# A four-layer network on one core: split subtractions on GpSimd, later transfers, and stages joined by halves

## The chip, the core and the metric

The kernel runs on one core of one Trainium2 chip. The metric is the device time of one execution in microseconds; lower is better. The engines are named as in the profile: PE (matrix products), PEld (its weight loads), DVE (VectorE), ACT (ScalarE), POOL (GpSimd) and SP, whose queue issues most transfers. All matrix products are float32 unless said otherwise.

## What is computed

The input x is 8 images of 256 channels of 32 x 32 pixels. Four layers follow, cut here to what matters:

```python
# layer 0: batch norm, attention over 1024 pixels (16 heads, key size 16, value size 64), MLP
q, k, v = wq @ bn(x) + bq, wk @ bn(x) + bk, wv @ bn(x) + bv
x = x + wp @ (softmax(q.T @ k * 4) @ v) + bp
x = x + w2 @ relu6(w1 @ bn(x) + bb1) + bb2
# layer 1: 1x1 convolution to 64 channels, deformable 3x3 convolution, 1x1 back
h = relu(bn(w1 @ x)); off, mask = split(conv3x3(h, woff) + boff)
h = bilinear(h, places + off) * sigmoid(mask)      # 9 taps of 4 corners
x = relu(bn(w3 @ relu(bn(w2 @ h))) + x)
# layer 2: sign(x) convolved 3x3 with sign(weights), batch norm over all images, added to x
x = x + bn(scaling * conv3x3(sign(x), sign(weights)))
# layer 3: conv3x3 to 128 channels, silu, depthwise 3x3, layer norm, gelu, offsets and masks,
#          deformable sampling of a 5x5 window, output product, silu, added to x
```

Batch norms of layers 0 and 2 need statistics over all images, so the stages are: attention, a middle stage (the MLP, layer 1 and layer 2's convolution), and layer 3.

## The kernel before, in words

x stays in SBUF as two tiles of 128 channels for 8 images of 1024 pixels; a half is 512 pixels.

**Attention.** Work goes by groups of four heads of an image (32 groups), each in two blocks of 512 queries, each block in NT = 8 steps of 128 keys. The order is written by hand: `plan(step, place, f, ...)` puts a piece of work into a step, and `step(t)` issues the scores and exponentials of the next keys (`exps`), the value products and sums of exponentials (`attend`; the additions of esum run on POOL), four score maxima of a later block (`score_max`: a product into a bank pb, then a DVE reduction), and the planned work of places 0, 1 and 2. The maxima use products of bfloat16 parts: `project_qk` computes u, the queries or keys of one half, and its first level lev; `split` makes the rest (stage 0), the second level (stage 1, ACT) and the third (stage 2), and writes each to DRAM; `stack` reads them back as rows of sq and sk. It is done for i = 0 to 3, the halves in the order of QK, in every second group. u has two buffers, lev four, pb two, e six. `total` sums the exponentials, copies the sums to a row and reads them back 16 to a partition (L494); `invert` takes the reciprocals and writes them to DRAM (L499); `lay` spreads them (L506) and `scale` applies them on POOL (L511). `bias` folds the bias of v into that of the output (L305), in two pieces at steps -6 and -4, among the first maxima of `score_max_first` (L422). PE, ACT, DVE and POOL run in the order written; SP's order is made by the framework.

**Middle stage.** A planner, `Order`, is given pieces with an engine, a duration, a rank (lower goes first), predecessors and buffers from rings that a piece takes or gives; it emits them in the order of its own simulated times. For each image b: `hidden` (L758), `relu6`, `mlp_out` (L771) and `mlp_add` are the MLP by halves; `reduced` and `reduced_relu` the 1x1 convolution; `table` and `table_write` write h four times, shifted, to DRAM as rows of four corners; `offsets`, `places`, `places_mask` and `places_cells` give cells and weights of the sampling; `gather` reads 9 x 128 rows by indirect DMA on POOL (L891) for each of 8 tiles of pixels, into three buffers g; `near_weights` and `sample` (L913, L917) blend them on DVE; `turn` and `turn_copy` (L937, L939) transpose them into st; `contract` (L948), `expand` (L958) and their additions finish layer 1. `sign` and `convolve` (L978) are layer 2's convolution, with one bank pc for images 0 to 6, its statistics (L985) and the sums stored to acc_d as 16-bit integers. `signs` prepares layer 2's weights. The last image's convolution starts when all of its pixels are there.

**Layer 3.** Its weights wc (1.2 MB) and its constants are loaded and computed first, in program order (L1101 to L1134), then a second `Order` runs: `load`, `normed3` (L1176), `add_normed` (L1180) and `border` (L1183) bring an image with layer 2's norm into xpad, `convolve3` (L1188) follows, and ten `spread_rows` pieces (L1165, L1167) make selection matrices, ranked 60.

Of the kernel before, what the change touches and what calls it, by code (L numbers as in the profile page):

```python
# [18 lines left out]
P = 128  # L19
# [139 lines left out]
def conv_seq_kernel(ctx: ExitStack, tc: tile.TileContext, d: dict, out: bass.AP):  # L159
# [76 lines left out]
    with ExitStack() as s0:  # L236
# [58 lines left out]
        def bank():  # L295
            return ps_p.tile([P, 512], F32, name="pb")
# [55 lines left out]
        def split(b, g2, i, stage):  # L352

            which, h = QK[i]
            u, rest, lev = parts[i]
            if stage == 0:
                nc.vector.tensor_sub(rest, u, lev[0])
                return
            if lev[stage] is None:
                lev[stage] = lp.tile([P, HALF], BF16, name="lev")  # L360
            if stage == 1:
                nc.scalar.copy(lev[1], rest)
            else:
                nc.vector.tensor_sub(lev[2], rest, lev[1])
# [122 lines left out]
        def total(m):  # L487

            ps = totals(m)
            row = sp.tile([P, HALF], F32, name="r", bufs=1)  # L490
            nc.scalar.copy(row, ps)
# [4 lines left out]
        def invert(m):  # L496
            nc.vector.reciprocal(rows[m], rows[m])
            inv_d[m] = ld.tile([4, HALF], F32, name="inv_d")
# [89 lines left out]
        for n, m in enumerate(blocks):  # L588
# [7 lines left out]
            else:  # L596
                plan(t1_ + 3, 1, total, m)
                at = 6 if n + 2 == nblk else 8
                plan(t1_ + (5 if at == 6 else 6), 0, invert, m)
                plan(t1_ + at, 2, lay, m)  # L600
# [8 lines left out]
        for t in range(2):  # L609
            plan(2 * t - 6, 1, bias, t)  # L610
# [21 lines left out]
        with tc.manual_schedule(engines={mybir.EngineType.PE, mybir.EngineType.Activation, mybir.EngineType.DVE, mybir.EngineType.Pool}):  # L632
# [6 lines left out]
            nc.gpsimd.dma_start(bv, d["bv"].rearrange("(t p) -> p t", p=P))  # L639
            for i in range(4):  # L640
# [20 lines left out]
    acc_d = dram.tile([B, P, 2, N], I16, name="acc_d")  # L661
    scaling = const.tile([P, 2], F32, name="scaling")
    with ExitStack() as s1_:
        w = s1_.enter_context(tc.tile_pool(name="b_w", bufs=1))
        w1 = wide
        w2 = w.tile([P, 8, C], F32, name="w2")
# [51 lines left out]
        near_p = pw.tile([P, 512], F32, name="near_p")  # L718
        work = Order(y=2, pm=2, hid=10, po=1, pl=3, idx=2, wts=2, g=3, near=2, samp=2, pc=1, ac=2)
# [14 lines left out]
        def signs(t, i):  # L734

            if i == 0:
                pss["w", t] = gp.tile([P, 9, C], F32, name="g"), w.tile([P, C], F32, name=f"size{t}")
# [39 lines left out]
        def corners(pool, wpool, pos, mask, npts, order):  # L777
# [12 lines left out]
            nc.vector.tensor_scalar_min(low, low, float(H - 1))  # L790
            hi = over
# [4 lines left out]
            cell = pool.tile([P, NT, npts], F32, name="cell")  # L796
            nc.vector.scalar_tensor_tensor(cell, low[:, :, :, iy], float(PW), low[:, :, :, ix], ALU.mult, ALU.add)
# [6 lines left out]
            return cell, wts  # L804
# [11 lines left out]
        def reduced(b):  # L816
            ps = pss["r", b] = bank()
            for t in range(2):
                for h in range(2):
                    nc.tensor.matmul(ps[h * CB : (h + 1) * CB, :], c1[:, t, :], x[:, t, b, h * HALF : (h + 1) * HALF], start=t == 0, stop=t == 1)  # L820

        def reduced_relu(b, s):
# [942 lines left out]
```

## Time and profile before

| | us |
|---|---|
| median of 3 runs | 4542.85 |
| runs | 4538.98 to 4544.85 |
| the profiled execution's own time | 4529.35 |
| its span, first to last instruction | 4527.5 |
| attention (to the last output product) | about 2685 |
| middle stage (to layer 2's norm) | 2685 to 3859 |
| layer 3 | 3859 to 4527 |
| PE busy | 4008.4 (89%) |
| POOL busy | 3301.9 (73%) |
| DVE busy | 2863.6 (63%) |
| ACT busy | 1874.9 (41%) |

The profile is one execution; its time is set beside its own span, and the runs' median beside other medians. In its lines, "pb L406" is the tile that an instruction writes and its line in the code; "<-" names what ended a wait; "remote" or "another core or an unknown queue" is a wait whose end no recorded instruction explains.

### The profile page before, as it was taken

The page shows a single profiled execution, that of the slowest core. Times are in us where ns is not written, and L with a number is a line of the kernel's source. Part 1 is how long each engine was busy: PE and PEld are TensorE (multiplying, and loading weights), DVE is VectorE, ACT ScalarE, POOL GpSimd, SP SyncE. Part 2 cuts the span into 40 slices and gives each one's busy share as a digit, 9 for nine tenths or more (in the row PEclk, how much of TensorE's full clock was granted, in tenths as well). Part 3 has the DMA queues.
Part 4 walks back from the last instruction along what each step waited for, and adds up shares of the span by engine and source line. Part 5 has one row for each costly group of instructions (what it writes and reads, how often), then busy time and mean ns, then how long its engine had stood idle before and what let it go on. Part 6 is the DMA issues. An engine that isn't in the chain of part 4 may idle for free.

```text
span 4527.5 us, 59803 instructions
## 1 busy us (share of the span) xinstructions
PE 4008.4 (89%) x20879; PEld 1528.1 (34%) x20879; DVE 2863.6 (63%) x4984; ACT 1874.9 (41%) x3360; POOL 3301.9 (73%) x2011
## 2 busy tenths in 40 slices
PE   6999999999999999999999997767767757899976
PEld 2333333333333333333333333323223222344332
DVE  5666666666666666666666663455455444688885
ACT  2554555555555555555555541122212211534331
POOL 2889888888889888888888863455555453078787
PEclk8999999999999999999999998788888778999978
DMA  5222221121221222122122112222223222100000
GB/s 163 66 60 54 68 71 54 59 76 55 66 67 54 61 71 65 53 63 75 53 64 68 54 50 63 73 84 79 81 85 93 81 86 69 47 10 15 14 15 24
DMA packets 224358, 284.11 MB, mean 63 GB/s; under 512 B 104352, under 2 KB 134576, under 8 KB 223792
## 3 DMA queue, kind: packets, MB, share of 16 engines
q1 hardware_dynamic: 193488, 196.49, 15.0%
q0 software_dynamic: 28720, 77.90, 5.8%
q10 hardware_dynamic: 1840, 5.81, 0.3%
q8 instruction: 168, 2.75, 0.3%
q14 instruction: 142, 1.16, 0.1%
HBM read 214.10 MB, written 64.34 MB: 62 GB/s over the span
## 4 chain that ended last, share of the span: by engine, by line
PE 73%; DVE 6%; another core or an unknown queue 6%; POOL 5%; issue 5%; DMA 2%; ACT 2%; SPq 1%; DVEq 0%; POOLq 0%; ACTq 0%
PE av L463 18%; PE sc L451 11%; PE pb L406 11%; PE pb L389 5%; PE pb L541 5%; PE pm L758 4%; PE po L771 3%; PE pc L1188 3%; PE pb L333 2%; POOL part L1387 2%; PE pc L978 2%; PE pb L484 1%; POOL ws L1331 1%; PE pa L1379 1%
## 5 line engine op out<-in xcount | busy, mean ns | idle before, releaser
L410 DVE TENSOR_REDUCE pm<-pb 128x1 f32<-128x512 f32 x2016 | 1375.7, 688 | 799.2 <-PE pb L406 796.2
L473 POOL TENSOR_TENSOR esum<-esum,e 128x1024 f32<-128x1024 f32 x762 | 1808.7, 2405 | 58.7 <-ACT e L452 57.5
L452 ACT ACTIVATE e<-sc 128x512 f32<-128x512 f32 x2048 | 1056.9, 602 | 653.2 <-PE sc L451 647.4
L463 PE MATMUL av<-e,v 128*64 128x512 f32 x4096 | 1051.1, 593 | 0.0
L891 POOL DMA_INDIRECT g<-table,idx x576 | 550.0, 955 | 551.2 <-DVE near_p L913 253.9
L406 PE MATMUL pb<-sk,sq 128*64 128x512 bf16 x4032 | 769.0, 387 | 42.8 <-ACT u L346 19.8
L451 PE MATMUL sc<-q,k 32*128 32x512 f32 x4096 | 591.4, 641 | 0.0
L406 PEld LDWEIGHTS <-sq 128*64 128x64 bf16 x4032 | 247.6, 109 | 877.6 <-issue 844.6
L471 POOL TENSOR_TENSOR esum<-e 128x1024 f32<-128x1024 f32 x127 | 303.1, 2406 | 277.7 <-ACT e L452 277.7
L758 PE MATMUL pm<-y,wide 128*128 128x512 f32 x512 | 262.3, 657 | 141.3 <-ACT hid L763 112.4
L463 PEld LDWEIGHTS av<-e,v 128*64 128x64 f32 x4096 | 289.9, 137 | 239.9 <-issue 146.9
L1387 POOL TENSOR_TENSOR part<-part,pr 128x512 f32<-128x512 f32 x212 | 276.0, 1302 | 55.0 <-DVE pr L1370 43.9
L1370 DVE TENSOR_TENSOR pr<-pw,v 128x512 f32<-128x512 f32 x394 | 253.8, 682 | 61.7 <-POOL part L1387 31.8
L1188 PE MATMUL pc<-xpad,wc 128*128 128x512 f32 x576 | 276.4, 605 | 5.3 <-ACT h L1193 5.3
L771 PE MATMUL po<-hid,w 128*128 128x512 f32 x512 | 241.9, 618 | 5.1 <-issue 4.0
L541 PE MATMUL pb<-o,wp 128*64 128x512 f32 x1024 | 244.7, 597 | 0.5 <-DVE r L519 0.3
L451 PEld LDWEIGHTS sc<-q,k 32*128 32x128 f32 x4096 | 164.4, 183 | 231.1 <-issue 187.3
L389 PE MATMUL pb<-wide,y 128*64 128x256 f32 x2048 | 241.8, 379 | 0.0
L763 ACT ACTIVATE hid<-pm,vec 128x512 f32<-128x512 f32 x128 | 87.1, 686 | 311.8 <-PE pm L758 140.8
L765 DVE TENSOR_SCALAR hid<-hid 128x512 f32<-128x512 f32 x128 | 53.1, 432 | 253.1 <-ACT hid L763 222.3
L758 PEld LDWEIGHTS pm<-y,wide 128*128 128x128 f32 x512 | 104.0, 210 | 279.7 <-issue 153.1
L913 DVE TENSOR_TENSOR near_p<-g,near_p 128x320 f32<-128x320 f32 (+1 forms) x384 | 177.4, 462 | 13.2
(259 smaller groups left out, 3981.7 us busy)
## 6 DMA issues: line engine op xcount, KB each, us to landing
sq<-lev_d SPq DMA_DIRECT2D x512, 64.0 KB
r<-inv_d SPq DMA_DIRECT2D x252, 128.0 KB
sk<-lev_d SPq DMA_DIRECT2D x496, 64.0 KB
lev_d<-lev SPq DMA_DIRECT2D x180, 128.0 KB
u_d<-u SPq DMA_DIRECT2D x60, 256.0 KB
g<-table,idx POOLq DMA_INDIRECT x576
table<-v SPq DMA_DIRECT2D x32, 256.0 KB
out<-res SPq DMA_DIRECT2D x32, 256.0 KB
```

The costliest lines, as they stand in the source:

```text
L389: nc.tensor.matmul(ps[c * 64 : (c + 1) * 64, (mt % 2) * 256 : (mt % 2 + 1) * 256], ys[b][:, t, k0 : k0 + 64], wv[:, t, g * 256 : (g + 1) * ...
L406: nc.tensor.matmul(ps[c * 64 : (c + 1) * 64, :], sq[pair][:, c, q0 : q0 + 64], sk[pair][:, c, kh * HALF : (kh + 1) * HALF], start=True, st ...
L410: nc.vector.tensor_reduce(maxima[m][:, pair, qt, kh : kh + 1], ps, AX.X, ALU.max)
L451: nc.tensor.matmul(ps, k[r, kt * P : (kt + 1) * P], q[r, h * HALF : (h + 1) * HALF], start=True, stop=True)
L452: nc.scalar.activation(es[m, kt, j // 2][:, j % 2, :], ps, AF.Exp)
L463: nc.tensor.matmul(av[i * HD : (i + 1) * HD, :], vss[b, g][:, kt, j * HD : (j + 1) * HD], e[:, i, :], start=kt == 0, stop=kt == NT - 1,)
L473: eng.tensor_add(sums[m, pair], sums[m, pair], es.pop((m, kt, pair)))
L541: nc.tensor.matmul(ps[c * 64 : (c + 1) * 64, :], wp[:, 2 * g + i, o0 : o0 + 64], outs[(b, g, h), i], start=i == 0, stop=i == 1,)
L758: nc.tensor.matmul(ps, w1[:, t, i * P : (i + 1) * P], ys[b, h][:, t, :], start=t == 0, stop=t == 1)
L771: nc.tensor.matmul(pss["o", b, h, t], w2[:, j, t * P : (t + 1) * P], hids[b, h, j], start=j == 0, stop=j == 7)
L891: nc.gpsimd.indirect_dma_start(out=g[:, k, :], out_offset=None, in_=tables[b][:TR, :], in_offset=bass.IndirectOffsetOnAxis(ap=idxs[b][:, t ...
L1188: nc.tensor.matmul(S["c", b, h], wc[:, t, k, :], tap(xpads[t], k, H // 2, h * H // 2), start=t == k == 0, stop=t == 1 and k == 8,)
```

## The change

In the attention, stage 2 of `split` moves from DVE to POOL, and for the first group stage 0 too. `total` is cut into `total` and `narrow` (one step later, in place 2), `invert` into `invert` and `put` (in place 2 of the step ahead of `lay`). `bias` is issued ahead of the first projection.

In the middle stage, image 0's 1x1 convolution and table are made by halves, and its offsets go ahead of its table; `corners` is cut into `cells` and `corner_weights`, and `places_cells` into `places_add`, `places_cells` and `places_weights`, so that the gathers wait for the cells alone, and the mask is computed after the addition. The last image's contraction, expansion, signs and convolution go by halves; the first half's convolution is made but for what needs the next row (`convolve_upper`) and finished later. The convolutions of images 3 to 6 wait for the last product of the last image's MLP. w2 and layer 3's wc share one buffer, `kept`; wc and image 0's sums (ac0, in the place of the MLP's weights) are loaded during the middle stage.

In layer 3, the constants become the pieces `arrange` and `constants` behind image 0's last addition, the selection rows follow them, and a small `silu` activation is put behind image 0's second border. `group` stays in its place.

```diff
@@ split: engines
+            first = (b, g2) == (0, 0)
             if stage == 0:
-                nc.vector.tensor_sub(rest, u, lev[0])
+                (nc.gpsimd if first else nc.vector).tensor_sub(rest, u, lev[0])
                 return
...
-                nc.vector.tensor_sub(lev[2], rest, lev[1])
+                nc.gpsimd.tensor_sub(lev[2], rest, lev[1])
@@ total, narrow, invert, put
+        def narrow(m):
+            row = rows[m]
             rows[m] = sp.tile([P, 16], F32, name="r16")
...
+        def put(m):
             inv_d[m] = ld.tile([4, HALF], F32, name="inv_d")
@@ the plan of a block
                 plan(t1_ + 3, 1, total, m)
                 at = 6 if n + 2 == nblk else 8
+                plan(t1_ + 4, 2, narrow, m)
                 plan(t1_ + (5 if at == 6 else 6), 0, invert, m)
+                plan(t1_ + at - 1, 2, put, m)
                 plan(t1_ + at, 2, lay, m)
...
-        for t in range(2):
-            plan(2 * t - 6, 1, bias, t)
...
+            for t in range(2):
+                bias(t)
             for i in range(4):
                 project_qk(0, 0, i)
@@ shared buffers
+    kept = keep.tile([P, 18 * P], F32, name="kept")
+    wc = kept.rearrange("p (t k o) -> p t k o", t=2, k=9)
+    ac0 = wide[:, 0, :].bitcast(I16).rearrange("p (t n) -> p t n", t=2)
...
+        w2 = kept[:, 0 : 8 * C].rearrange("p (t o) -> p t o", o=C)
@@ image 0's first pieces
+            if b == 0:
+                for h in range(2):
+                    piece(("d", 0, h), "PE", 1.72, r, [("a", 0, h, t) for t in range(2)], reduced, 0, (h,), take=["pl"] * (1 - h))
+                    for i in range(2):
+                        piece(("dr", 0, i, h), "ACT", 0.8, r + i, [("d", 0, h), ("dr", 0, i - 1, h)], reduced_relu, 0, i, (h,), give=["pl"] * (h * i))
...
-            piece(("f", b), "PE", 4.3, r + 3, [("d", b, 1)], offsets, b, take=["pl"])
+            piece(("f", b), "PE", 3.2, r + 3 - 2 * (b == 0), ready[1], offsets, b, take=["pl"])
@@ places of every image (r = 100 * b - 50)
-            piece(("pm", b), "ACT", 0.5, r, [("p", b), ("pc", b - 1)], places_mask, b)
-            piece(("pc", b), "DVE", 5.5, r, [("pm", b)], places_cells, b, take=["idx", "wts"], give=["pl"])
+            piece(("pa", b), "DVE", 0.75, r - 400, [("p", b), ("pw", b - 1)], places_add, b)
+            piece(("pm", b), "ACT", 0.5, r, [("pa", b)], places_mask, b, give=["pl"])
+            piece(("pc", b), "DVE", 2.3, r - 400, [("pa", b)], places_cells, b, take=["idx"])
+            piece(("pw", b), "DVE", 2.3, r - 400, [("pc", b), ("pm", b)], places_weights, b, take=["wts"])
@@ the last image
+                piece(("k", b, h, i), "PE", 2.2 if h else 4.4, -400, after, contract, b, (h,), n0, n1, take=["pl"] * (1 - i))
...
+                piece(("x", b, t, h), "ACT", 0.6, -100, [("er", b, t, h)] + [("v", b - 2, o, h_) for o in range(2) for h_ in range(2)], sign, b, t, (h,))
...
+        def convolve_upper(b, o, rest):
+            if not rest:
+                pss["v", b, o, 0] = pm.tile([P, HALF], F32, name="pm")
+            rows = H // 2
+            taps = [(t, k) for t in range(2) for k in (range(6, 9) if rest else range(9))]
+            for n, (t, k) in enumerate(taps):
+                r0, r1 = (rows - 1, rows) if rest else (0, rows - (k > 5))
+                nc.tensor.matmul(
+                    pss["v", b, o, 0][:, r0 * W : r1 * W], ws[:, t, k, o * P : (o + 1) * P], tap(xbs[b % 2][:, t, :], k, r1 - r0, r0),
+                    start=bool(n == 0 and not rest), stop=bool(rest and n == len(taps) - 1),
+                )
...
+            piece(("vu", o), "PE", 3.9, 100 * b + 330, [("x", b, 0, 0), ("x", b, 1, 0), ("h", b, 1, 7)], convolve_upper, b, o, 0, take=["pm"])
...
+        piece("wc", "SP", 0.5, 0, [("o", B - 1, 1, t, 1) for t in range(2)], nc.sync.dma_start, wc, d["l3_wcv1"].rearrange("(t p) k o -> p t k o", p=P))
+        piece("ac0", "SP", 0.5, 0, [("h", B - 1, 1, 7)] + [("vd", 0, o, h) for o, h in halves], nc.sync.dma_start, ac0, acc_d[0])
@@ layer 3
+                piece("arrange", "DVE", 1.7, 20, [("a", 0, 1, 1)], arrange)
+                piece("constants", "DVE", 2.0, 20, [("a", 0, 1, 1)], constants)
+                for i in range(SB):
+                    piece(("sel", i, 0), "DVE", 0.4, 60, ["constants"], spread_rows, i, 0, take=["spread"])
...
+                piece("silu", "ACT", 0.2, r, [("xp", 0, 1)], nc.scalar.activation, silu_in, eps, AF.Silu, kind="silu")
```

## The prediction

> **What bounds the kernel now.** I read the page's busy digits first, then busy time by stretches, then TensorE's waits in the attention, then the timelines there, then the waits of the middle stage, and last the chain.
>
> ```profile
> PE   6999999999999999999999997767767757899976
> POOL 2889888888889888888888863455555453078787
> PEclk8999999999999999999999998788888778999978
> 200.00:1000.00 800.00, 786.05 (x5020) 281.48 (x5018) 528.29 (x856) 423.94 (x797) 699.68 (x314) 1.00 0.22 63
> 2900.00:3000.00 100.00, 67.49 (x219) 28.00 (x218) 52.39 (x116) 21.32 (x37) 52.55 (x55) 0.80 0.28 80
> ```
>
> One slice is 113 us. Slices 1 to 23 are the attention: PE is busy 786 of 800 us at full clock, so no more than 1.7% can be taken from it. The middle stage (about 2690 to 3858 us) has PE at two thirds and no full engine: it is bound by waits. Layer 3 follows from 3859.
>
> ```profile
> PE pb L406 <- ACT u L346: 19.1, 14, 1.4
> PE pb L406 <- DMA sk<-lev_d: 10.2, 7, 1.8
> PE pb L406 <- DMA sq<-lev_d: 9.7, 7, 1.5
> PE pb L406 <- DMA q<-u_d: 1.3, 1, 1.3
> ```
>
> These are all of PE's idle waits from 200 to 2640 us (total, times, longest): 40.3 us, twice per 162.6 us, the period of two groups of heads. One period shows both:
>
> ```profile
> 962.79 24.53 POOL L473 TENSOR_TENSOR esum<-esum,e 128x1024 f32<-128x1024 f32 x10
> 982.24 2.87 DVE L364 TENSOR_TENSOR lev<-u,lev 128x512 bf16<-128x512 f32 x1
> 985.20 0.69 ACT L346 ACTIVATE u<-pb,bq 128x512 f32<-128x512 f32 x1 [3.95 <-DVE lev L364]
> ...
> 1012.15 2.47 SPq L494 DMA_DIRECT2D r<-r  x4
> 1018.09 0.41 PE L406 MATMUL pb<-sk,sq 128*64 128x512 bf16 x2 [1.44 <-DMA sq<-lev_d]
> ```
>
> First, the third level of half 1 is subtracted on DVE in 2.87 us, ScalarE needs its buffer u for half 3, and PE soon needs the bank that ScalarE empties. Second, SP waits for the row of sums, then issues its four narrow reads (L494), and the stacks sk and sq behind them come 1.4 us late.
>
> ```profile
> POOL g L891 <- DVE near_p L913: 253.9, 25, 23.9
> ACT hid L763 <- remote: 116.2, 11, 22.9
> POOL g L891 <- DVE hid L765: 80.2, 1, 80.2
> DVE pos L883 <- ACT mask L878: 40.9, 4, 14.2
> ```
>
> In the middle stage the 64 gathers of 11.3 us run from 2770.65 to 3791.65: 717 us busy, 304 us of pauses, mostly because DVE has not freed a buffer g. DVE is late because results of PE reach ScalarE and DVE up to 23 us late ("remote") while gathers run back to back. What delays them I cannot see; it ends when the gathers pause. The chain gives the two ends:
>
> ```profile
> 69.39 3.50 PE pb L305 x16
> 78.94 3.50 PE pb L305 x16
> 3837.34 17.73 PE pl L978 x72
> 3855.07 6.31 issue
> 3870.78 2.00 PE pc L1188 x2
> 3872.99 15.54 PE pc L1188 x34
> ```
>
> At the start two bias products stand between the first score maxima. At 3837 the last image's whole convolution (72 matmuls) comes after its last pixel; layer 3 then needs until 3873 for its own first convolution.
>
> [...]L364 takes 0.80 us at best, but 2.87 us where a POOL addition of 2.36 us began 0.03 us before it. [...]the trace's 128x512 float32 product (L511) takes 1.25 to 1.32 us. No row shows it with bfloat16. [...]I use the trace's times.
>
> **The change, part by part.**
>
> *Start.* Each bias product leaves DVE without a reduction for 4.2 us (70.70 to 74.92, 80.26 to 84.48): 8.4 us go. They move into PE's idle 7.6 us ahead of L333 at 37.01. wp's last packets start at 15.9 us. Their two banks come free at 31.2 (the ScalarE copies of bq4 and bk), and their DVE additions stand behind the four y (38.2): the first projection starts up to 1.5 us later; I take 1.0. The first group's eight subtractions go to POOL: about 1.3 us each, ahead of the loads of q and k on that queue, which end near 49 instead of 47.8, and are needed at 53. DVE's first maximum gains 1.1 us (55.0 to 53.9). The third levels come some 1 us later, at 56, and are read by PE after 75. **Gain 8.5 us**; 4 to 10.
>
> *Third level on POOL, 60 times.* In POOL's queue it stands behind the two additions of its step. For half 1 those end at 982.25 (in 13 of 15 periods within 0.05 us of DVE's start). Before it POOL now also does half 0's (+1.27)[...]; so it ends at 982.25 + 1.27 - 0.65 + 1.27 = 984.15 instead of 985.11. ScalarE's u comes some 0.9 us earlier: of PE's 1.36 us stall 0.45 stays, **gain 14 x 0.9 = 13 us**. Bounds: free of any wait, 19; at 2.0 us an operation, -8. Halves 2 and 3 get earlier (POOL is free at 987.3 and 1003.7; DVE ended at 995.6 and 1006.7), which helps the stacks. Behind it on POOL stand the two scalings, needed five steps later, and additions; POOL goes from 87% to about 92%, and its 4 to 5 us of idle per block pay that.
>
> *Narrow reads and put later.* The four L494 (2.5 us of SP) go behind that step's stacks, the put behind the next ones. The six stack transfers behind them come 2.5 us and the wait for the row earlier: the 1.44 us go whole. Behind narrow on SP stand a maximum's line and the other pair's stacks, which are two steps from use; lay waits for put's landing, with two steps to the scaling. **Gain 20 us**; none if SP's order does not follow.
>
> *Middle stage, first image.* The chain from its last addition (2751.2) to the first gather (2770.65) is 19.4 us: product 1.9, four ScalarE copies 3.2, transposes 0.8, offsets 2.9, copies and transposes 2.5, table load and sigmoid 1.6, DVE 4.1, with gaps. By halves two copies are left (-1.6) and half the product (-0.9); transposes go behind the offsets (-0.7); the mask is off the path (-2.2); the gather waits only for the cells (-2.0). The table's second part lands earlier than that. **Gain 8 us** if later gathers move with it; 0 to 10.
>
> *Later images.* The pieces places_add, places_cells and places_weights get rank -400 below their image, ahead of sampling (-200). DVE's wait for the mask (40.9 us) can go; DVE may also wait at places_add for PE. I take **0**, from -35 (faster) to +40.
>
> *Last image by halves.* From the last copy of st (3823.6) to layer 2's norm (3858.92) are now 35.3 us. After: a quarter of the contraction 1.3, relu 0.7, expansion and addition 1.2, four half copies and signs 2.4 to 2.6, two rests of the upper half 1.0, two lower convolutions 8.5, statistics and norm 4.2: 19.4. **Gain 16 us.** The upper half's 8.4 us of PE lie in PE's idle beside sampling; without that cover they come back.
>
> *Layer 3's start.* From the norm to the steady convolution are 13.9 us: weights wc queued at 3858.4, DVE's constants, copies waiting for wom until 3867. After: wc (1.2 MB) and image 0's sums (0.5 MB) are loaded beside the gathers (DMA share 0.3); ScalarE 0.86, DVE 0.70, again 0.86 overlapped, border 1.05: 3.6. **Gain 10.3**, and 1.3 for the table load at 3888.6. On SP the two loads wait for the last MLP product; behind them stand sums of convolutions that now wait for the same. The constants and selections, about 10 us of DVE, lie beside 31 us of convolution; without that cover they delay the depthwise part.
>
> **Sum** 8.5 + 13 + 20 + 8 + 0 + 16 + 11.6 = 77 us. The profiled execution took 4529.35 us (span 4527.5); so 4452 there. The median 4542.85 is 0.3% above it; 4542.85 - 77 = **4466 us**.
>
> **Rivals.** (1) *The attention's gain fails in part*: SP keeps its order or POOL's subtraction is slow. For: SP is not in the list of hand-ordered engines. Against: narrow is later in program order. 4466 + 20 to 35: about 4492. It includes that the transfers do not move at all. (2) *The middle stage gains too*: the mask waits and the 34.6 us that image 6's gathers wait for idx go: 35 us more, 4431. Against: pauses are also when PE's late results arrive. (3) *Slower: DVE stands at places_add.* It now outranks sampling; if PE's transposes are then late, sampling queues behind it and g stays full. Place: images 1 to 7. Price: the waits of DVE for remote results, 72.6 us over 8, 9 us each, up to 23. From 77 / 7 = 11 us per image it decides; at 13 it gives 4557. Against: mask waits show that DVE already stands there.
>
> **How the numbers follow.** Chances: the sum 0.55 (own range 4440 to 4500), rival 1 0.13, rival 2 0.10, rival 3 0.22, of which 0.05 ends within 0.2% (9 us, about what a measurement can tell from no change). So faster 0.78, same 0.05, slower 0.17. Leaving out the top 0.13 and a little below: 4425 to 4553.
>
> **Right or wrong.** PE's waits at L406 should fall from 40 to below 12 us and the period from 162.6 to about 160.3; POOL's L364 should take 1.2 to 1.4 us; L305 stand ahead of 39 us; the first gather come about 11 us after image 0's last addition instead of 19; the stretch from the last gather to layer 3's convolution shrink from 81 to about 54 us. It would be wrong if the gathers' pauses, 304 us, changed by more than 40, or ScalarE's u waited more than 4 us for POOL.

## The result and the profile after

The changed kernel is slower: 4593.44 us median of four runs (4587.29 to 4605.76) against 4542.62 (4538.98 to 4544.85), ratio 1.0116, interval 1.0093 to 1.0139. The profiled execution took 4605.76 us, its span is 4603.88. The stage marks of the two profiles, in us from the start of the span:

| mark | before | after | difference |
|---|---|---|---|
| first value product | 98.92 | 91.83 | -7.1 |
| last output product of the attention | 2685.15 | 2749.84 | +64.7 |
| first gather | 2770.65 | 2833.29 | +62.6 |
| last gather's end | 3791.65 | 3887.75 | +96.1 |
| layer 2's norm | 3858.92 | 3944.94 | +86.0 |
| layer 3's first convolution | 3870.73 | 3949.03 | +78.3 |
| end | 4527.46 | 4603.88 | +76.4 |

The attention loses 72 us between the first and the second line; the joints between the stages gain, and the stretch of gathers loses 33. The page's busy digits hardly show it (one slice is 115 us):

```profile
PE   7999999999999999999999998676677766899977
POOL 3889889888888889888988982554554544068787
PEclk8999999999999999999999999887888877999978
```

Busy time by stretches shows more (length, then busy time and instructions of PE, PEld, DVE, ACT and POOL, the granted clock, the DMA share, GB/s):

```profile
200.00:1000.00 800.00, 787.96 (x4912) 280.76 (x4910) 493.43 (x822) 417.11 (x781) 699.04 (x327) 0.98 0.21 60
2900.00:3000.00 100.00, 62.94 (x206) 28.32 (x205) 44.08 (x108) 15.18 (x30) 51.22 (x54) 0.81 0.29 84
```

PE is as busy as before (788 of 800 us), but with 4912 products instead of 5020, and at a clock of 0.98 instead of 1.00. A busy PE is not one that gets on. PE's waits from 200 to 2640 us, all of them:

```profile
PE sc L453 <- DMA q<-line: 39.9, 14, 3.1
PE sc L453 <- ACT e L454: 0.7, 1, 0.7
```

The 40 us at L406 (now L408) are gone, as the change intended, and 40 us of another wait stand there: the scores of the exponentials wait for the line, the row of maxima that `enter_max` sends to q. One of the fourteen, in the chain of waits (start, length, what):

```profile
1169.19 1.17 POOL lev L366
1170.36 0.02 issue
1170.38 0.32 SPq L367
...
1170.79 1.74 DMA q<-line
1172.53 0.14 issue
1172.67 4.19 PE sc L453 x8
```

SP's timeline at the same place:

```profile
1160.10 0.33 SPq L349 DMA_DIRECT2D lev_d<-lev  x1
1160.76 9.94 SPq L367 DMA_DIRECT2D lev_d<-lev  x2
1170.79 2.82 SPq L441 DMA_DIRECT2D q<-line  x4
```

DVE finished the line well before that:

```profile
1163.27 0.86 DVE L434 STREAM_TRANSPOSE line<-nm 32x32 f32<-32x32 f32 x4
```

SP could not send it at 1164.13: two writes of levels (L367) stand ahead of it in its queue, and the second is that of the third level, for which SP waits until POOL has made it at 1170.35. In the kernel before, the same line went out as soon as DVE had it, and the third level's write followed behind it:

```profile
977.39 2.83 SPq L439 DMA_DIRECT2D q<-line  x4
985.13 0.34 SPq L365 DMA_DIRECT2D lev_d<-lev  x1
```

The framework, which orders SP's queue, puts the write first once its subtraction is POOL's. The line lands at 1172.53, and PE has waited 2.82 us.

### The profile page after: what moved, and what is told of

It reads as the page before. It is cut to its first block, busy times and chain, and to the rows that moved or that the text cites. A ratio compares the mean times of both kernels' runs of the same rounds, so it can differ in the third digit from the quotient of the medians.

```text
span 4603.9 us, 59779 instructions
## 1 busy us (share of the span) xinstructions
PE 4087.4 (89%) x20901; PEld 1552.0 (34%) x20901; DVE 2782.0 (60%) x4916; ACT 1882.9 (41%) x3366; POOL 3349.5 (73%) x2079
## 3 DMA queue, kind: packets, MB, share of 16 engines
q1 hardware_dynamic: 193408, 196.49, 14.7%
q14 instruction: 142, 1.16, 0.1%
## 4 chain that ended last, share of the span: by engine, by line
PE 73%; another core or an unknown queue 6%; POOL 6%; DVE 6%; issue 6%; ACT 2%; DMA 1%; SPq 0%; DVEq 0%; POOLq 0%; ACTq 0%
PE av L465 19%; PE sc L453 13%; PE pb L408 11%; PE pb L391 5%; PE pb L548 5%; PE pc L1300 3%; PE pm L774 3%; PE po L787 3%; PE pb L333 2%; POOL part L1499 2%; PE pc L1022 2%; PE pb L486 1%; DVE near_p L951 1%; PE pw L1473 1%
## 5 line engine op out<-in xcount | busy, mean ns | idle before, releaser
L475 POOL TENSOR_TENSOR esum<-esum,e 128x1024 f32<-128x1024 f32 x762 | 1788.7, 2379 | 63.4 <-ACT e L454 63.0
L465 PE MATMUL av<-e,v 128*64 128x512 f32 x4096 | 1068.2, 603 | 0.0
L408 PE MATMUL pb<-sk,sq 128*64 128x512 bf16 x4032 | 774.4, 391 | 1.9 <-DVE pm L412 1.6
L453 PE MATMUL sc<-q,k 32*128 32x512 f32 x4096 | 637.8, 653 | 43.2 <-DMA q<-line 42.5
L408 PEld LDWEIGHTS <-sq 128*64 128x64 bf16 x4032 | 246.4, 110 | 860.4 <-issue 845.5
L787 PE MATMUL po<-hid,kept 128*128 128x512 f32 x512 | 260.1, 658 | 77.3 <-DVE x L791 73.2
L1300 PE MATMUL pc<-xpad,kept 128*128 128x512 f32 x576 | 276.5, 604 | 11.5 <-DMA bom<-in_l_bom 7.9
L453 PEld LDWEIGHTS sc<-q,k 32*128 32x128 f32 x4096 | 186.5, 186 | 288.9 <-issue 196.0
L774 PE MATMUL pm<-y,wide 128*128 128x512 f32 x512 | 244.6, 624 | 20.6 <-issue 11.2
L395 ACT COPY v<-pb 128x512 f32<-128x512 f32 x128 | 74.9, 585 | 267.3 <-PE pb L391 267.3
L955 DVE TENSOR_TENSOR samp<-samp,near_p 128x320 f32<-128x320 f32 (+1 forms) x384 | 174.0, 453 | 15.1 <-DVE near_p L951 1.9
```

The source lines that it names most:

```text
L408: nc.tensor.matmul(ps[c * 64 : (c + 1) * 64, :], sq[pair][:, c, q0 : q0 + 64], sk[pair][:, c, kh * HALF : (kh + 1) * HALF], start=True, st ...
L453: nc.tensor.matmul(ps, k[r, kt * P : (kt + 1) * P], q[r, h * HALF : (h + 1) * HALF], start=True, stop=True)
L465: nc.tensor.matmul(av[i * HD : (i + 1) * HD, :], vss[b, g][:, kt, j * HD : (j + 1) * HD], e[:, i, :], start=kt == 0, stop=kt == NT - 1,)
L475: eng.tensor_add(sums[m, pair], sums[m, pair], es.pop((m, kt, pair)))
L774: nc.tensor.matmul(ps, w1[:, t, i * P : (i + 1) * P], ys[b, h][:, t, :], start=t == 0, stop=t == 1)
L787: nc.tensor.matmul(pss["o", b, h, t], w2[:, j, t * P : (t + 1) * P], hids[b, h, j], start=j == 0, stop=j == 7)
```

## Experiments

The chips are of two kinds: the kernel before takes 4529 to 4543 us on some and 4209 to 4212 on others. Most of the difference (297 of 318 us) lies in the stretch from the first gather to the last: 1021 us in the first profile, 724.5 in a profile of the kernel before on the other kind. Whether it is the chip itself or something that lasted on it is not shown. In the attention they agree: its last output product ends at 2685.15 and 2683.03. So each ratio is to the kernel before on the same chip, and the marks and periods of the attention can be compared across all. "Period" below is the mean time of two groups, from the value products of block 8 to those of block 60; it is 162.8 us for the kernel before and 167.3 for the changed one (162.76 and 162.85, 167.29 and 167.36 in their two profiles).

| run | us | before, same chip | ratio (interval) | period |
|---|---|---|---|---|
| after_again | 4600.57 | 4540.45 | 1.0136 (1.0119 to 1.0153) | 167.4 |
| after_dve | 4149.92 | 4209.04 | 0.9856 (0.9839 to 0.9872) | 161.1 |
| before_pool | 4291.89 | 4209.04 | 1.0200 (1.0183 to 1.0217) | 168.3 |
| before_later | 4186.76 | 4209.04 | 0.9946 (0.9929 to 0.9962) | 161.2 |
| after_write | 4137.05 | 4209.04 | 0.9825 (0.9809 to 0.9841) | 160.0 |
| dve_write | 4505.94 | 4540.45 | 0.9924 (0.9908 to 0.9941) | 161.0 |
| after_line | 4173.54 | 4208.92 | 0.9911 (0.9895 to 0.9928) | 162.1 |
| wait_2 | 4581.88 | 4539.60 | 1.0094 (1.0063 to 1.0125) | 166.4 |
| wait_6 | 4593.98 | 4539.60 | 1.0113 (1.0080 to 1.0146) | 167.6 |
| wait_10 | 4610.48 | 4539.60 | 1.0153 (1.0121 to 1.0186) | 168.9 |
| late_two_queues | 4238.23 | 4212.40 | 1.0064 (1.0047 to 1.0081) | 167.2 |
| short_two | 4528.35 | 4528.73 | 0.9997 (0.9978 to 1.0015) | 163.6 |
| mid_only | 4533.94 | 4540.45 | 0.9984 (0.9971 to 0.9997) | 162.9 |
| attn_only | 4494.43 | 4539.60 | 0.9897 (0.9866 to 0.9928) | 160.0 |
| write_rank | 4490.58 | 4540.45 | 0.9891 (0.9874 to 0.9907) | 160.0 |
| before_again | 4208.98 | 4208.92 | 1.0001 (0.9992 to 1.0010) | 162.8 |
| write_nogate | 4135.47 | 4208.92 | 0.9826 (0.9809 to 0.9842) | 160.0 |
| write_mask | 4137.39 | 4208.92 | 0.9829 (0.9812 to 0.9845) | 160.0 |

### Which part of the attention: one at a time

after_dve, the changed kernel with the subtraction back on DVE:

```diff
-                nc.gpsimd.tensor_sub(lev[2], rest, lev[1])
+                (nc.gpsimd if first else nc.vector).tensor_sub(lev[2], rest, lev[1])
```

> The changed kernel with the third level of every group but the first subtracted on DVE again; all else as changed. Theory A (place in SP's queue): with the subtraction on GpSimd, SP's write of the third level stands ahead of the maximum's line and holds it; here the line goes out right after DVE made it, PE's waits for q<-line fall from 40 to below 3 us, the last output product ends near 2665 us instead of 2749.8, and the run takes about 4510 (4495 to 4530). Theory B (the later transfers cost the time, not GpSimd): it stays above 4570. Theory C (GpSimd's subtraction slows the additions of exponentials by itself): same time as A, but PE's wait for q<-line would be replaced here by nothing, and it would not come back when only the write's queue is changed.

before_pool, the kernel before with that subtraction alone on GpSimd:

```diff
-                nc.vector.tensor_sub(lev[2], rest, lev[1])
+                nc.gpsimd.tensor_sub(lev[2], rest, lev[1])
```

> The kernel before with only the third level of split (stage 2, all 64 subtractions) moved to GpSimd. Theory A: the 2.8 us waits of PE for q<-line appear 14 times, the period of two groups grows from 162.6 to about 167, and the run takes about 4610 (4590 to 4625), 65 us above the kernel before. Theory B: GpSimd's subtraction alone is worth the predicted gain of 13 us: about 4530.

before_later, the kernel before with `narrow` and `put` as in the change and nothing else:

```diff
+                plan(t1_ + 4, 2, narrow, m)
                 plan(t1_ + (5 if at == 6 else 6), 0, invert, m)
+                plan(t1_ + at - 1, 2, put, m)
```

> The kernel before with only the narrow reads and the put of the reciprocals issued later. Theory A: the transfers are harmless and the stack waits of PE (about 20 us in all, up to 1.44 us, 14 times) go: about 4525 (4515 to 4540). Theory B: they cost the attention's time: about 4600. If the cycle of two groups is set by something else than these two waits, no change: 4543.

after_again is the changed kernel unaltered.

> The changed kernel as it is, so that its stages can be set beside those of the other kernels on one chip. If the attention alone carries the loss (14 waits of 2.85 us for q<-line and the slow clock after them), it stands 45 to 60 us above the kernel before, and its middle stage, from the first gather to the last, is as long as that of the kernel before; if the middle stage carries part of it, the gathers' stretch is 20 us or more longer and the ratio is above 1.014.

after_again stands 60 us above the kernel before and its stretch of gathers is 1040.8 us, 20 us longer than in the first profile: both lie on the edge between the two alternatives, so that this run decides neither.

The two changes of the attention have opposite signs. GpSimd's subtraction alone costs 83 us (65 were expected) and brings the new wait; PE's waits in before_pool begin with

```profile
PE sc L451 <- DMA q<-line: 40.8, 14, 3.5
```

The later transfers alone gain 22 us: all waits for stacks are gone. With the subtraction on DVE the attention ends at 2653.26 us (expected near 2665) and the run is 59 us below the kernel before, not above it. These runs show that the subtraction's move is the cause; they do not yet show whether it is POOL's work or SP's queue.

### POOL's work or SP's queue

after_write leaves the subtraction on GpSimd and issues the write of the third level from ScalarE's queue, whose order is written by hand, a step later:

```diff
-            nc.sync.dma_start(lev_d[b, g2][which, stage, :, h * HALF : (h + 1) * HALF], lev[stage])
+            if first or stage == 1:
+                write(b, g2, i, stage)
+
+        def write(b, g2, i, stage):
...
+            eng = nc.scalar if stage == 2 and (b, g2) != (0, 0) else nc.sync
+            eng.dma_start(lev_d[b, g2][which, stage, :, h * HALF : (h + 1) * HALF], lev[stage])
...
                     plan(t0 + (11, 14, 16, 18)[i], 0, split, b_, g2, i, 2)
+                    plan(t0 + (12, 15, 17, 19)[i], 0, write, b_, g2, i, 2)
```

> The changed kernel, the third level still on GpSimd, but its write to DRAM issued from ScalarE's queue one step later (for the first group still from SP), so that nothing on SP waits for GpSimd. Theory A: SP issues the line right after DVE's transposes, PE's waits for q<-line fall below 3 us, and the attention ends near 2665 us or somewhat earlier than with the subtraction on DVE: about 4505 (4490 to 4530). Theory C (GpSimd's subtraction is the cost, by delaying the additions): still above 4575, with another wait of PE in its place.

dve_write is its control: the same write from ScalarE's queue, with the subtraction on DVE.

> The changed kernel with the third level on DVE (but for the first group) and its write issued from ScalarE's queue one step later: the control of the run with GpSimd and ScalarE's queue (4137). If GpSimd's subtraction itself gives the 13 us that were predicted (u free 0.9 us earlier, 14 times), this run shows PE waiting 1.3 us for ScalarE's u 14 times and takes 10 to 15 us longer than that run, about as long as the run with everything on DVE and SP. If the gain came from moving the write off SP, it takes the same time as the run with GpSimd.

after_line leaves the write on SP and moves the line instead:

```diff
-                nc.sync.dma_start(row.rearrange("o (q p) -> o q p", p=src.shape[1]), src)
+                nc.scalar.dma_start(row.rearrange("o (q p) -> o q p", p=src.shape[1]), src)
```

> The changed kernel with the four transfers of each maximum's line issued from ScalarE's queue; the third level stays on GpSimd and its write on SP, still waiting there. If the loss is the line's place behind that write, PE's waits for q<-line fall below 5 us, SP still waits about 200 us for the third level, no stretch of half clock is left between 200 and 2600 us, and the attention ends where it ends with the write moved instead (about 2637 us, 112 us earlier than in the changed kernel), some us later where ScalarE waits for DVE's line. If the late write itself (and what it delays: stacks) were the loss, the time stays within 10 us of the changed kernel's.

after_write beats both kernels: it takes 1.75% less than the kernel before, and only two variants of it, below, equal that. Its waits of PE from 200 to 2640 us begin with

```profile
PE pb L415 <- ACT u L346: 2.9, 14, 0.2
```

that is, PE now waits 0.2 us for u where it waited 1.4. The control keeps this wait:

```profile
PE pb L415 <- ACT u L346: 17.7, 13, 1.4
```

Its period is that of after_dve (161.05 and 161.07), 1.0 us above after_write (160.02). So what after_write gains on after_dve (14 periods of 1.05 us make 14.7; the medians differ by 12.9) comes from the subtraction on GpSimd and not from the other queue.

In after_line SP still waits for the third level,

```profile
SPq L367 <- POOL lev L366: 214.7, 42, 9.3
```

but nothing of use stands behind that wait: PE's waits are 3.1 us in all (200 to 2640 us), and the granted clock over the run is 0.974, as in after_write, whose clock is 1.00 from 200 to 2600 us. The period fell by 5.2 us of the 7.3; the attention ended at 2677.9, where about 2637 and some was expected. The 2.1 us a period that are left are in the scores: they keep PE busy for 38.6 us a period instead of the 36.6 of after_write, while each other kind of product takes as long in both to 0.02 us. ScalarE, which now sends the line, waits for DVE's maxima,

```profile
ACT e L454 <- DVE pm L412: 216.4, 50, 5.5
```

which it never does in after_write; that this is what pulls the scores apart is likely, not shown. Both runs show the cause of the loss: the line's place behind the third level's write.

### What a late line costs

The 14 waits of 2.85 us make 40 us, but the changed kernel's period is 7.3 us above after_write's. To measure the price alone, the line of one block in four is made late in after_write, by k copies of it onto itself on ScalarE (k is 2, 6 or 10):

```diff
+            if n % 4 == 3 and n > 3:
+                hooks[n * NT - 2, 3] = m, line
...
+            for i in range(2):
+                nc.scalar.copy(line, line)
+            send(m, line)
```

> The changed kernel with the third level's write on ScalarE's queue (no waits of PE left), and, in one block of four from the eighth on, the maximum's line copied onto itself by ScalarE two times, ahead of its fourth exponential of the step before the line is used, so that the line goes out late by a chosen time; 15 such blocks. By my estimate PE then waits about 1 us each time. If a wait costs only its own length, the attention gets 15 times the wait longer (about 15 us) and the granted clock stays 1.00; if the clock falls after any wait, 4 to 5 us more each.

> As with two copies, but six: PE should wait about 2 us each time. [...]some of the 15 waits are followed by half clock and some not, and the cost lies between 2 and 6.5 us each[...].

> As with two copies, but ten: PE should wait about 3 us each time. If the wait and the clock after it are the whole price of the line that came late in the changed kernel, each wait costs about 7.3 us[...], the attention ends 100 to 115 us later than without the copies, as it does in the changed kernel; if GpSimd's subtraction had another cost besides, it ends earlier than in the changed kernel by that cost.

late_two_queues is wait_6 with two of the late line's four transfers from ScalarE's queue; short_two is the same with one copy. The lines in time keep SP's queue for all four:

```diff
+            send(m, line, nc.scalar)
...
+        def send(m, line, second=nc.sync):
...
-                nc.sync.dma_start(row.rearrange("o (q p) -> o q p", p=src.shape[1]), src)
+                (second if j % 2 else nc.sync).dma_start(row.rearrange("o (q p) -> o q p", p=src.shape[1]), src)
```

> As with six copies of the line, but the late line's four transfers go out from two queues, two from SP and two from ScalarE's, so that the four rows land within some 0.7 us instead of 2.1. With one queue each late line cost 7.5 us a time: 2.7 of wait and 4.8 beyond it, the same 4.8 to 5.0 that waits of 1.36 and 3.98 us had beyond their length. If that surcharge is the line's rows landing one after another (the scores of four heads then run one by one, 4.2 us instead of 1.1) and the clock falling over a stretch of such products, the scores take about 2 us, the surcharge falls to 1 to 3 us and the half-clock stretches get rarer: the attention ends 25 to 55 us earlier than with one queue. If the surcharge comes with any late line, because of the wait alone, it ends within 8 us of it.

> One copy of the line only, so that PE waits about 1.4 us, and the late line's four transfers from two queues as before. With one queue a wait of 1.36 us was followed by half clock 14 times in 14, in windows in which PE idled about 1 us and then ran the scores of one head after another (3.9 us for what takes 1.1 side by side). If it is that stretch of products of 32 rows that lets the clock fall, it falls seldom here and a late line costs 1.5 to 4 us, so that the attention ends 35 to 65 us earlier than with one queue (2730); if a wait ahead of the scores is enough, it falls each time and costs 5.5 to 6.5 us.

The price is the period less after_write's 160.0:

| kernel | wait each, us | price, us | beyond the wait |
|---|---|---|---|
| before (two waits a period, at L406) | 1.4 and 1.4 | 2.8 | 0 |
| after | 2.85 | 7.3 | 4.4 |
| wait_2 | 1.35 | 6.4 | 5.0 |
| wait_6 | 2.69 | 7.5 | 4.8 |
| wait_10 | 3.98 | 8.9 | 4.9 |
| late_two_queues | 3.01 | 7.1 | 4.1 |
| short_two | 1.33 | 3.5 | 2.2 |

With one queue a late line costs its wait and 4.4 to 5.0 us more, at waits of 1.35 to 3.98 us. The copies on ScalarE are not what costs this: it is the same with two of them and with ten. The waits came out longer than was expected (1.35, 2.69 and 3.98 us for about 1, 2 and 3), and so did the prices of wait_6 (7.5 us, where 2 to 6.5 were named) and wait_10 (the attention ends 133 us later than in after_write, where 100 to 115 were named). PE's timeline in wait_2 (its score products alone; in brackets the idle time before them and what ended it) and the busy time by stretches of 3.4 us show where the surcharge is:

```profile
1189.76 1.14 PE L475 MATMUL sc<-q,k 32*128 32x512 f32 x8
1194.96 3.90 PE L475 MATMUL sc<-q,k 32*128 32x512 f32 x8 [1.36 <-DMA q<-line]
```

```profile
1192.80:1196.20 3.40, 2.04 (x9) 0.79 (x6) 1.64 (x4) 0.78 (x3) 3.40 (x2) 1.00 0.01 2
1196.20:1199.60 3.40, 3.40 (x10) 1.05 (x10) 0.13 (x1) 2.33 (x4) 2.63 (x2) 0.67 0.33 84
1199.60:1203.00 3.40, 3.40 (x10) 0.82 (x8) 1.25 (x2) 0.00 (x0) 0.00 (x0) 0.50 0.29 80
```

The scores of four heads, 32 rows of the array each, usually run side by side: eight products in 1.14 us. Behind a late line each head's row comes with its own transfer, the four sent within 2.8 us, and the heads run one after another: 3.90 us. Then the granted clock is half (0.50) for 3.4 or 6.8 us, after each of the 14 late lines up to 2600 us (its mean from 200 to 2600 us is 0.98, in after_write 1.00). By an estimate from these lines, the scores are 2.8 us of the 5.0, part of that at half clock already, and the clock after them the rest. None of this is in the list of waits: PE is busy.

With two queues and a short wait, the scores take 2.34 us:

```profile
1186.22 2.34 PE L475 MATMUL sc<-q,k 32*128 32x512 f32 x8 [1.36 <-DMA q<-line]
1194.20 1.14 PE L475 MATMUL sc<-q,k 32*128 32x512 f32 x8
```

Half clock still follows 11 of the 14 times, where it was expected seldom, but ten of them for 3.4 us only (the mean from 200 to 2600 us is 0.99), and the price falls from 6.4 to 3.5 us, within what was expected (the attention ends 39 us earlier than in wait_2). Behind a wait of 3.0 us two queues help little, against the expectation of 25 to 55 us: the scores take 2.8 to 3.0 us instead of 4.2, but half clock followed each time, for 6.8 us (mean 0.98), and the attention ends 5 us earlier. So the one-by-one scores are a large part of what a short wait costs beyond its length (one pair of runs, wait_2 and short_two, shows it); behind the longer waits the clock fell whether the scores ran one by one or in pairs. What exactly makes the clock fall is not shown by these runs.

### The middle stage and layer 3

mid_only is the kernel before in the attention with the change's other stages; attn_only is after_write's attention with the other stages of the kernel before; write_rank, write_nogate and write_mask are after_write with one part of the middle stage undone:

```diff
@@ write_rank (the same for places_cells and places_weights)
-            piece(("pa", b), "DVE", 0.75, r - 400, [("p", b), ("pw", b - 1)], places_add, b)
+            piece(("pa", b), "DVE", 0.75, r, [("p", b), ("pw", b - 1)], places_add, b)
@@ write_nogate
-... [("x", b, 0), ("x", b, 1), ("p", b + 4) if b < 3 else ("o", B - 1, 1, 1, 1)], convolve ...
+... [("x", b, 0), ("x", b, 1), ("p", min(b + 4, B - 1))], convolve ...
@@ write_mask: mask before the addition, all at their image's rank, gathers behind the weights
-... NT * b + t, [("pc", b), ("tw", b, 1)], gather ...
+... NT * b + t, [("pw", b), ("tw", b, 1)], gather ...
```

> The kernel before in the attention (third level on DVE and SP, narrow and put early, bias among the first maxima), with the change's middle stage and layer 3. By the stage marks so far: first gather 2 to 4 us earlier, last image 12, layer 3's start 8 + 1: 20 to 26 us below the kernel before (ratio 0.994 to 0.995). If places ahead of sampling cost time (rival 3), the gathers' stretch grows and it ends near the kernel before or above it.

> The attention of the changed kernel with the third level's write on ScalarE's queue, and the middle stage and layer 3 of the kernel before. If the parts add, it takes 47 us less than the kernel before (4162 where that takes 4209, 4493 where it takes 4540). Where the kernel before takes about 4540 and its stretch of gathers is shorter than the change's by 20 us or more, it comes out at 4493 or below, no slower than the run with the change's middle stage there (4490); if the middle stage of the change is a gain there too, 10 to 20 us slower than that.

> The changed kernel with the third level's write on ScalarE's queue, and places_add, places_cells and places_weights ranked with their image instead of 400 below it. If rival 3 is right, DVE no longer stands at places_add and the gathers' stretch gets shorter by 20 us or more; if the rank does nothing, because GpSimd's gathers are back to back, the time is that of the same kernel with the changed rank (4137 where the kernel before took 4209, ratio 0.983) within 8 us; if the early rank helps, it is longer.

> The kernel before, for a second set of stage marks. Where the chip is one on which it takes about 4540, the stretch from the first gather to the last is 1021 us as in the first profile if that is its usual length, so that the change's middle stage (1041 to 1060 us in five profiles) is longer by itself; 1040 to 1060 if the first profile was a short one. Where it takes about 4210, the stretch is about 725 us as with the changed kernel.

> The changed kernel with the third level's write on ScalarE's queue, and the convolutions of images 3 to 6 waiting for places of image b + 4 or the last (as before) instead of the last product of the MLP. If that gate pushes four convolutions behind the last gathers and is what lengthens the stretch of gathers (image 7's by 10 us), the stretch is 10 to 20 us shorter than with the gate and the last image's tail no longer than 57 us; if not, it is within 8 us of it.

> The changed kernel with the third level's write on ScalarE's queue, and the places of every image as before: the mask first, then addition, cells and weights in one go at their image's rank, and gathers behind the weights. If standing at places_add (83 us of waits of DVE for PE) is what lengthens the stretch of gathers, it is 15 to 35 us shorter than with the split; if the wait for the mask only takes its place, it is within 10 us, and the first gather comes about 3 us later.

Lengths from the profiles, in us:

| stretch | before | with the change's stages |
|---|---|---|
| first MLP product to first gather | 79.8 to 81.4 | 77.0 to 78.4 (write_mask 79.6) |
| first gather to last, chips with 4529 to 4543 | 1021.0, attn_only 1037.2 | 1040.7 to 1060.4, nine profiles |
| the same, chips with 4209 to 4212 | 724.5 to 726.1 | 723.9 to 724.8 |
| last gather to layer 2's norm, first kind | 67.3, attn_only 68.9 | 50.8 to 57.2 |
| the same, second kind | 44.3 to 45.4 | 29.7 to 32.2 |
| norm to layer 3's third product | 13.9 | 5.95 |

On the second kind of chip the gathers follow one another without pause, and no variant moves them. In before_again POOL's waits there begin with the 0.3 us between the nine instructions of a gather, with the idle time ahead of the first gather (80.5 us), and with waits for a free buffer g, which are as short as the others:

```profile
POOL g L891 <- issue: 159.3, 523, 0.3
POOL g L891 <- DVE hid L765: 80.8, 2, 80.5
POOL g L891 <- DVE near_p L913: 6.7, 22, 0.3
```

On the first kind the stretch is 4 to 39 us longer in each of the nine profiles with the change's middle stage than in the two with that of the kernel before, which differ by 16 us themselves. This takes back most of the gain of the joints: mid_only is 6.5 us faster where 20 to 26 were expected. In the changed kernel the waits of POOL and DVE there (2833 to 3888 us) are

```profile
POOL g L929 <- DVE near_p L951: 303.0, 25, 25.2
DVE x L791 <- remote: 146.7, 11, 19.3
DVE pos L915 <- PE pl L902: 80.2, 5, 27.8
```

The wait for the mask (40.9 us before) is gone and DVE waits 80.2 us for PE in the same place; but with the rank undone it waits 83.2 us there and the stretch is 1060.4. The rank is not the reason. write_nogate and write_mask ran on chips where the stretch grew in no run, so whether one of those parts lengthens it stays open, as does what delays PE's results on the first kind of chip. On the second kind the two parts are worth nothing measurable: after_write, which has both, takes 4137.05 us, write_nogate 4135.47 and write_mask 4137.39. attn_only came out as expected (-45 us for -47).

## Why the prediction was wrong

**Start**: 8.5 us predicted, 7.1 measured at the first value product; the bias products stand at 31.6 to 38.2 us, ahead of 39. Right.

**Third level on POOL**: 13 predicted, 12.9 to 14.7 measured (after_write against after_dve, by medians and by periods). The subtraction takes 1.16 us, u waits at most 2.8 us for it, PE's wait for u falls to 0.2. Right as a price, and yet this is the step that failed. It followed the moved instruction through POOL's queue and named what stands behind it there; it did not follow the write that the same call issues (L365, now L367) through SP's queue. Its bounds, 19 and -8, were those of POOL's speed. What was needed was at hand: the prediction has POOL's end at 984.15 (the 0.65 us taken off in it was the author's estimate; in the trace before, a POOL addition beside half 0's L364 took 2.81 us and others 2.35, 0.46 us less), and in the trace before the scores that need the line start ahead of that:

```profile
983.45 1.14 PE L451 MATMUL sc<-q,k 32*128 32x512 f32 x8
```

With the write ahead of the line, SP's 0.4 and the transfer's 1.74 (both from the trace after) bring the line to 986.3, 2.85 us late, which is the measured wait; 14 times, 40 us. The list of right and wrong signs had u, L408 and the gathers, and no line for q. Without the late line the part does what was said of it: the period named was 160.3 us, after_write's is 160.0.

**Rival 1** said that SP might keep its order or POOL be slow, and priced this as the gain that fails, 20 to 35 us. SP changed its order instead, and in the wrong direction.

**The price of a wait** was taken as its length. This held for the waits at L406 (2.8 us a period for 2.8 us of waits) and not for a late line: 7.3 us for 2.85. Fifteen late lines a run (the 14 listed and one at 167 us) at 7.3 us are 110 us; less 7.1 of the start, 22.3 of the later transfers and 14.7 of GpSimd, that is a loss of some 65 us, where 64.7 was measured.

**Narrow reads and put later**: 20 predicted, 22.3 measured alone. Right.

**Middle stage, first image**: 8 predicted, 1 to 4 measured. After the last addition the chain took 13.7 us (predicted 11, before 19.4), but the addition itself came 2 to 4 us later, probably since the first half's product and table now stand in PE's order ahead of the MLP; no run takes this apart. The mis-sized term is "half the product (-0.9)": four products of one half take 1.86 us and the eight of both took 1.87. The two halves had run side by side.

**Later images**: taken as 0 with -35 to +40. 0 on one kind of chip, +4 to +39 on the other. The bounds held; rival 3 named the right stretch and a reason that the rank's run speaks against.

**Last image by halves**: 16 predicted, 12.5 measured in the changed kernel: from the last copy of st to the norm 35.3 us became 22.8 (22.4 to 25.2 in all profiles with the change). From the last gather's end the gain is 10 to 18 us on the first kind of chip and 12 to 16 on the second. Chain of the changed kernel's tail:

```profile
3921.80 3.80 PE pl L988 x10
3925.62 0.78 ACT h L994
...
3931.11 0.39 PE pm L1036 x9
3931.50 9.59 PE pl L1022 x36
3941.12 0.71 DVE stats L1042
```

The last copy of st ends at 3922.1, and 19.4 us were predicted from there. "A quarter of the contraction 1.3" is 3.5, because the quarter before it ran only then too; relu, expansion, addition and signs take 5.5 instead of 4.4. The rest, 13.8 us from 3931.1 on, was put at 13.7.

**Layer 3's start**: 11.6 predicted, 9 measured (13.9 to 5.95, and 1.0 in the first image's convolution). The 3.6 us was the time to the first product (4.1), not to the steady row that the 13.9 was measured to.

So the sum of the gains priced one by one was 77 us; after_write, which keeps them all without the late line, gains 72 where the gathers run without pause. On the first kind of chip, for which the forecast was made, the nearest run (write_rank) gains 50, since the longer stretch of gathers takes some 20 us back. The forecast failed by one wait that the change makes elsewhere; without it the gain would still have been short of 77 us there.

## What to carry to other kernels

When an instruction moves to another engine, follow what it issues as well. Here a write that waited in SP's queue until 1170.35 us held the line behind it, made by 1164.13, until 1170.79; and the framework had put the write ahead of the line with the move, where it stood behind it before (985.13 against 977.39 us). Put such a write into a queue with nothing urgent behind it: from ScalarE's the period was 160.0 us instead of 167.3. Do not price a wait of PE at its length before a run has shown it: behind waits of 1.35 to 3.98 us it was the length and nearly 5 us more here. And compare periods and instruction counts, not busy shares.

## What the runs showed of the hardware

- **Half clock followed waits of 1.35 us.** In wait_2, waits of 1.35 us, followed by scores of one head after another (3.90 us), were followed by half clock 14 times in 14. Waits of 1.2 to 1.5 us ahead of the products at L406 were not once in the kernel before (27 of them), and with 14 such waits in before_later the mean clock from 200 to 2600 us is 1.00; of the two longer ones in the kernel before, 1.81 and 1.83 us, one was, for 3.4 us. So the length of a wait alone does not tell these apart.
- **Half clock came in multiples of 3.41 us.** From 200 to 2640 us it lasted 3.41 us in the kernel before (once, from 853.9 us) and 10.24 or 6.83 us in the changed one (once and 13 times). There, from 504.3 us on, it began every 167.25 us (1006.0, 1173.3, 1340.5 and so on), twelve times in a row; that is 49 times 3.41 us. That this holds the changed kernel's period at 167.3 us is not shown.
- **Products that share the array.** Eight score products of 32 rows take 1.14 us side by side, and 3.90 (wait_2) to 4.19 us (the changed kernel) where the heads ran one after another, part of that at half clock. Four products of the first image's half take 1.86 us and the eight of both took 1.87: splitting these saved nothing.
- **Chips differ.** The same kernel's stretch of gathers took 1021 us on one kind of chip and 724.5 on the other, with the end of the attention within 2.1 us.
